# Zero fills of a results' array, two per iteration of the first attention and each behind that iteration's reciprocal

## The chip, the cores and the metric

The kernel runs on one core of a Trainium2 chip. The time is the device time of one execution in microseconds (us), and the median of several executions is compared. Before the change it is 1532.57 us, the median of three runs (1531.0 to 1534.91).

The engines go by short names. PE is the matrix engine TensorE, and PEld its weight loads. DVE is VectorE, ACT is ScalarE, POOL is GpSimd. SP is the engine that issues the plain DMA transfers here, and SPq is its queue of instructions. Each engine carries out its own instructions in order; engines wait for each other through semaphores.

## The reference, cut to what matters

The model has two layers, each an attention over another sequence and then a mixture of 8 experts in which every token goes to its two best ones. The batch has 64 entries of 128 tokens with 128 features.

```python
x = x + L0_xattn(layernorm(x), fside, memory_k=ctx, memory_v=ctx)   # 16 heads of 8, keys: 128 + 120
x = x + L0_ffn(layernorm(x))          # router, top 2 of 8 experts, silu(a) * g @ w2
x = x + L1_xattn(layernorm(x), ctx, ctx)                            # 16 heads of 8, keys: 120
x = x + L1_ffn(layernorm(x))          # router, top 2 of 8 experts, gelu
...
# the first mixture of experts
for e in range(E):
    he = silu(a) * g @ w2[e].T
    out = out + where(expert_ids == e, he, 0)
combined = (out * scores).reshape(N, TOP_K, h).sum(axis=1)
```

Everything is computed in 32-bit floats.

## The kernel before, in words

**Stages.** The profile's first 640 us are the first attention. Then come some 350 us in which the first mixture of experts is worked off in 71 tiles of 256 rows (NTL is 71), and then the second attention, with the second mixture of experts woven in.

**The first attention.** One iteration `it` handles one batch entry at each of several stages: maxima of the scores for entry `it` (L394 on PE, L414 on DVE), the scores again and their exponentials for entry `it - 2` (L430 on PE, L438 on ACT), the values for entry `it - 3` (L475), and the division and output projection for entries `it - 3` to `it - 5`. Near the end of an iteration `out2` (L487) turns the values of one entry round on PE (L491), takes the reciprocals of the sums on DVE (L495) and multiplies (L497). So there is one such reciprocal in each iteration from `it = 3` on. In each iteration PE does all the L394 and L430 products before the turn at L491.

**Groups and loads.** Four entries make a group `g`. The key tiles `K2` exist twice, for even and odd groups. The context half of the keys of group `g` is written there by two loads at L261 of 240 KB each, in the program at iteration `4(g-1) + 2`. It overwrites what group `g - 2` used, and group `g - 2` is last read by the L394 and L430 products of iteration `4(g-1) + 1`. It is first read by L394 in iteration `4g`. The context half of the values follows at L266 (960 KB), and the next source of keys and values, `kvT`, at L256 (256 KB).

**The results' array.** `ys` lies in the chip's main memory and takes the results of the 71 expert tiles (L1135), which are later gathered by row (L1157, L1360). Before that, each of its 71 pieces of 256 rows is filled with zeros from the tile `zero` by a DMA of 128 KB (L1278). `Aside0.end`, called last in every iteration, writes two such fills into the program from `it = 4` to `it = 39`.

**The order of work.** PE, ACT, DVE and POOL work in the order in which the program was written. In the first attention's first 62 iterations this isn't so for SP:

```python
with tc.manual_schedule(engines=ORDERED):    # L1328; ORDERED: PE, ACT, DVE, POOL
    for _ in range(B - 2):
        next(steps)
```

There the framework's planner sets SP's order before the kernel runs. It goes by when, on its own estimate of times, the things that a transfer waits for are done. On the chip SP then keeps to that order: a transfer that waits holds all later ones. In the last iterations (L1331) SP's order too is as written. The framework finds most waits from the tiles that an instruction reads and writes. The tile `zero` is set once at the start, and `ys` isn't read or written by anything before the fills, so that the fills before the change wait for nothing in the attention.

Of the kernel before, what the change touches and what calls it, by code (L numbers as in the profile page):

```python
# [23 lines left out]
HD = 8  # L24
# [20 lines left out]
def transformer_kernel(ctx, tc, a, out):  # L45
    nc = tc.nc
# [185 lines left out]
    def attention(layer, w, norm, first, aside):  # L232
# [5 lines left out]
        with ExitStack() as es:  # L238
# [37 lines left out]
            def mtile():  # L276
                return banks.tile([128, 512], F32, name="bank", tag="bank")
# [209 lines left out]
            def out2(b):  # L487
                ov = ots.pop(b)
                pt = mtile()
                for v in range(NV):  # L490
                    nc.tensor.transpose(pt[:, v * 128 : (v + 1) * 128], ov[:, v * S : (v + 1) * S], ident)  # L491
                pt = pt[:, : NV * 128].rearrange("q (h w) -> q h w", w=16)
                rs = stat.tile([S, H], F32, name="rs", tag="rs")
                aside.probe = rs[0:1, 0:1]
                nc.vector.reciprocal(rs, pt[:, :, HD])  # L495
                o = rows.tile([S, H, HD], F32, name="o", tag="o")
                nc.vector.tensor_tensor(  # L497
                    o, pt[:, :, 0:HD], rs.unsqueeze(2).to_broadcast([S, H, HD]), ALU.mult
                )
                pts[b] = o  # L500
# [52 lines left out]
            for it in range(B + 5):  # L553
# [21 lines left out]
                if first:  # L575
# [13 lines left out]
                    rounds(2, 3)  # L589
                    on(4, out3)  # L590
                    on(3, out2)
                    prep(it, 1)
                    aside.end(it, work, mtile)
                else:
# [5 lines left out]
                    prep(it, 0)  # L600
                    on(4, out3)
                    on(3, out2)
                    on(5, out4)
                    aside.call(it, mtile)
# [20 lines left out]
    class Router:  # L625
# [22 lines left out]
        def rest(self, mtile):  # L648
            self.mtile = mtile
            self.t = 1 << 20  # L650
            while min(self.due) < 1 << 30:
                self.call(None, mtile)
# [52 lines left out]
        def best(self, lg, n, l):  # L705
# [26 lines left out]
            nc.vector.tensor_scalar(cap, one1, -BIG, BIG / 2.0, ALU.mult, ALU.add)  # L732
            rest = tl("rest", n)
            nc.vector.tensor_tensor(rest, lg, cap, ALU.min)
            nc.vector.tensor_reduce(m2, rest, AX.X, ALU.max)
            yield 0
            one2 = first_at(rest, m2, "one2")
            yield 0
            e2 = tl("e2", n, 1)
# [503 lines left out]
    class Aside0(Ahead):  # L1243
# [29 lines left out]
        def end(self, it, work, mtile):  # L1273

            for t in range(2 * (it - GB), 2 * (it - GB) + 2):

                if 0 <= t < NTL:
                    nc.sync.dma_start(  # L1278
                        ys[t * TT : (t + 1) * TT].rearrange("(h p) d -> p h d", p=S), zero[:, :, :D]
                    )  # L1280
            if it == B - 2:
                self.tiles = tile_stage(work, mtile)
            if it >= B - 2:
                next(self.tiles)

        def rest(self, mtile):
            for _ in self.tiles:
                pass


    wr0 = const.tile([D, 3 * E], F32, name="c_wqkvT", tag="c_wqkvT")
# [270 lines left out]
```

## Time and profile before

| What | us |
|---|---|
| median of three runs | 1532.57 |
| the profiled execution's own time | 1582.29 |
| its span, first to last instruction | 1580.5 |
| PE busy | 1442.8 (91% of the span) |
| DVE busy | 1106.3 (70%) |
| ACT busy | 849.7 (54%) |
| POOL busy | 641.3 (41%) |

The profiled execution is 3.2% longer than the median of the unprofiled runs. Times of rows are counted from the span's start. A row names the line, the engine, the operation, the tile that it writes and those that it reads. For a DMA issued by SP the row gives the time that SP spent on issuing it; the transfer itself runs on afterwards. A wait is put down to the work whose end came last. The granted clock of PE (PEclk) is a share of full speed.

### The profile page before, as it was taken

What the parts mean: (1) busy time and instruction counts of PE and PEld (TensorE: products, weight loads), DVE (VectorE), ACT (ScalarE), POOL (GpSimd) and SP (SyncE); (2) the same over time, 40 slices, a digit from 0 to 9 for tenths busy, and PEclk for the clock granted to TensorE, in tenths of its full rate; (3) what the DMA queues carried; (4) which work ended last, traced back from release to release, by engine and by line L of the source; (5) the groups of instructions that cost most, each with busy time, mean ns of one, the idle gap of its engine ahead of it and who ended that gap; (6) DMA issues with size and microseconds to landing.
All of it is one profiled execution on the core that took longest, in us unless ns stands there. A gap on an engine that the chain in (4) does not pass through costs nothing.

```text
span 1580.5 us, 41996 instructions
## 1 busy us (share of the span) xinstructions
PE 1442.8 (91%) x16620; PEld 1118.6 (71%) x16620; DVE 1106.3 (70%) x3024; ACT 849.7 (54%) x1740; POOL 641.3 (41%) x1195
## 2 busy tenths in 40 slices
PE   7969999999999999787999999888989898988987
PEld 5757777777777677676888888566666676666765
DVE  6757888888888988354654444688776777777763
ACT  4646666666666666442333333566656565655653
POOL 4122345646465534464001122376555555444210
PEclk9989999999999999899999999899999999999999
DMA  7851222222222221365776676111000111100000
GB/s 192 222 138 46 55 61 68 67 61 64 57 64 58 56 70 37 93 187 173 213 201 189 194 202 180 46 35 30 28 28 28 37 31 31 31 28 15 15 8 28
DMA packets 143719, 133.03 MB, mean 84 GB/s; under 512 B 48546, under 2 KB 126114, under 8 KB 141602
## 3 DMA queue, kind: packets, MB, share of 16 engines
q1 hardware_dynamic: 135330, 113.02, 25.9%
q0 software_dynamic: 8192, 17.32, 3.5%
q8 instruction: 132, 2.16, 0.6%
q14 instruction: 65, 0.53, 0.1%
HBM read 97.32 MB, written 32.97 MB: 82 GB/s over the span
## 4 chain that ended last, share of the span: by engine, by line
PE 66%; DVE 15%; DMA 6%; SPq 5%; issue 3%; ACT 3%; POOL 3%; another core or an unknown queue 0%; POOLq 0%; ACTq 0%; DVEq 0%
PE bank L430 10%; PE bank L475 9%; PE bank L1115 8%; PE bank L394 8%; PE bank L1420 4%; PE bank L1441 4%; DVE nm L414 3%; PE bank L1128 3%; DMA q<-xs 3%; SPq L1278 2%; PE bank L407 2%; PE bank L292 2%; DVE q L462 2%; PE bank L511 2%; PE bank L681 2%
## 5 line engine op out<-in xcount | busy, mean ns | idle before, releaser
L414 DVE TENSOR_REDUCE nm<-bank 128x2 f32<-128x496 f32 (+1 forms) x768 | 465.4, 662 | 100.6 <-PE bank L430 68.6
L438 ACT ACTIVATE p<-bank 120x512 f32<-120x512 f32 (+1 forms) x768 | 403.5, 603 | 154.9 <-PE bank L430 138.5
L430 PE MATMUL bank<-q,k 32*120 32x256 f32 (+1 forms) x3072 | 444.5, 401 | 14.8 <-DVE nm L414 5.0
L430 PEld LDWEIGHTS bank<-q,k 32*120 32x120 f32 (+1 forms) x3072 | 298.3, 182 | 61.9 <-DVE nm L414 16.6
L394 PE MATMUL bank<-k,q 32*128 32x248 f32 x2048 | 294.3, 403 | 12.5 <-DMA k<-in_ctx_k 11.8
L394 PEld LDWEIGHTS bank<-k,q 32*128 32x128 f32 x2048 | 203.1, 190 | 59.7 <-issue 23.0
L475 PE MATMUL bank<-p,v 128*32 128x128 f32 (+1 forms) x4096 | 179.6, 279 | 1.8 <-DVE h L1435 0.6
L1120 DVE TENSOR_TENSOR p<-p,bank 128x256 f32<-128x256 f32 x213 | 87.9, 420 | 125.4 <-ACT p L1119 112.6
L407 PE MATMUL bank<-k,qf 32*128 32x480 f32 x512 | 150.8, 604 | 1.3 <-ACT qf L295 0.8
L807 POOL DMA_INDIRECT xs<-xn,at x128 | 129.2, 1009 | 28.6 <-issue 25.0
L1119 ACT ACTIVATE p<-bank 128x256 f32<-128x256 f32 x213 | 80.9, 384 | 100.9 <-PE bank L1115 91.9
L484 ACT COPY ov<-bank 128x256 f32<-128x256 f32 x128 | 48.0, 375 | 157.5 <-PE bank L475 146.0
L475 PEld LDWEIGHTS bank<-p,v 128*32 128x32 f32 (+1 forms) x4096 | 111.2, 110 | 26.1 <-issue 13.2
L1115 PE MATMUL bank<-q 128*128 128x256 f32 x516 | 122.3, 388 | 4.6 <-ACT q L1106 4.6
L1360 POOL DMA_INDIRECT yb<-ys,back x112 | 108.7, 970 | 27.7 <-issue 19.3
L462 DVE SCALAR_TENSOR_TENSOR q<-bank,c_smask,q 128x256 f32<-128x256 f32 x256 | 111.1, 475 | 10.3 <-PE bank L459 9.6
L167 POOL TENSOR_SCALAR xn<-x,mv,rstd 128x128 f32<-128x128 f32 x252 | 110.6, 452 | 7.3 <-issue 1.3
L1115 PEld LDWEIGHTS bank<-q 128*128 128x128 f32 x516 | 97.4, 196 | 17.3 <-ACT q L1106 5.0
L155 POOL TENSOR_SCALAR rstd<-mv 128x4 f32<-128x4 f32 x32 | 6.4, 199 | 246.7 <-DVE mv L113 150.0
L475 PE MATMUL bank<-p,vc 120*32 120x128 f32 x2048 | 104.2, 272 | 0.6 <-issue 0.5
L1157 POOL DMA_INDIRECT kvT<-ys,back x16 | 15.4, 962 | 197.5 <-DMA vc<-xs 118.1
L301 ACT ACTIVATE q<-bank,c_a_bq,c_hmask 128x512 f32<-128x512 f32 x124 | 90.1, 788 | 9.8 <-PE bank L292 9.8
(224 smaller groups left out, 2477.6 us busy)
## 6 DMA issues: line engine op xcount, KB each, us to landing
q<-in_w SPq DMA_DIRECT2D x43, 576.0 KB
vc<-in_w SPq DMA_DIRECT2D x28, 576.0 KB
vc<-in_ctx_v SPq DMA_DIRECT2D x16, 960.0 KB
ys<-zero SPq DMA_DIRECT2D x71, 128.0 KB
k<-in_ctx_k SPq DMA_DIRECT2D x32, 240.0 KB
q<-xs SPq DMA_DIRECT2D x43, 128.0 KB
ys<-q SPq DMA_DIRECT2D x43, 128.0 KB
x<-in_x SPq DMA_DIRECT2D x16, 256.0 KB
```

The source lines that it names most:

```text
L167: nc.gpsimd.tensor_scalar(xn[:, j, :D], xg[g][:, j, :], self.mv[:, b, 0:1], self.rstd[:, b : b + 1], ALU.add, ALU.mult,)
L301: nc.scalar.activation(q4s[g][:, :, s, :], pq.rearrange("p (b q) -> p b q", b=GB), AF.Identity, bias=w["bq"][:, s : s + 1], scale=hmask[:, ...
L394: nc.tensor.matmul(pa[:, u, :], lhsT=q4s[g][r, j, s, :], rhs=k2[g % 2][r, s // 2, j, :], start=True, stop=True,)
L407: lambda: nc.tensor.matmul(pa, lhsT=qfs[g][r, j, :], rhs=k4s[g][r, :, j, :], start=True, stop=True),
L414: nc.vector.tensor_reduce(nm[b % 2].rearrange("q i (a s) -> q a i s", s=16)[:, 2 * ra + v : 2 * ra + v + len(slots) // 2, :, 0], pa.rearra ...
L430: nc.tensor.matmul(pb[:n, v * 256 : (v + 1) * 256], lhsT=k2[g % 2][r, v, j, k0 : k0 + n], rhs=q4s[g][r, j, 2 * v : 2 * v + 2, :].rearrange ...
L438: nc.scalar.activation(ps_[b][:n, c, ra, :], pb[:n], AF.Exp, scale=SCALE)
L462: nc.vector.scalar_tensor_tensor(q, pm, smask[:, v : v + 1], q, ALU.mult, ALU.add)
L475: nc.tensor.matmul(pav[32 * ra : 32 * ra + 32, v * S : (v + 1) * S], lhsT=vs[g % 2][c][:, j, 4 * v + ra, i, :], rhs=p[:n, c, ra, (2 * v + ...
L807: s = nc.gpsimd.indirect_dma_start(xs, bass.IndirectOffsetOnAxis(at[:, j, k : k + 1], 0), xn, None)
L1115: nc.tensor.matmul(ph[:, u, :], lhsT=w[:, c, u * 128 : (u + 1) * 128], rhs=xT, start=True, stop=True)
L1360: nc.gpsimd.indirect_dma_start(y[:, k, b % 2, :], None, ys, bass.IndirectOffsetOnAxis(back[:, b, k : k + 1], 0),)
```

## The change

The reciprocal of `out2` is remembered in `aside.pace`. Each fill of `ys` is given a dependency on the reciprocal remembered last, which is that of its own iteration, since `out2` comes before `end` in an iteration. The fills, their number, their sizes and their place in the program stay as they are. The dependency is of the kind that puts a real wait into the program.

```diff
@@ out2 @@
                 aside.probe = rs[0:1, 0:1]
-                nc.vector.reciprocal(rs, pt[:, :, HD])
+                aside.pace = nc.vector.reciprocal(rs, pt[:, :, HD])
@@ Aside0.end @@
                 if 0 <= t < NTL:
-                    nc.sync.dma_start(
+                    z = nc.sync.dma_start(
                         ys[t * TT : (t + 1) * TT].rearrange("(h p) d -> p h d", p=S), zero[:, :, :D]
                     )
+
+                    tc.add_manual_dep(z.ins, self.pace.ins.name, AFTER, reason="spread")
@@ after the class @@
+    AFTER = mybir.DependencyInfo(mybir.DependencyClass.Sync, mybir.DependencyReason.DATA)
```

## The prediction

> **What bounds the kernel now.** I read the stretches first, to see which engine fills the first attention and where it doesn't. Columns: busy us of each engine (instructions), granted clock, DMA share, GB/s.
>
> ```profile
> 40.00:84.00 44.00, 42.08 (x651) 31.25 (x642) 30.94 (x68) 28.51 (x58) 5.46 (x14) 0.96 0.80 218
> 84.00:96.00 12.00, 0.36 (x4) 0.39 (x8) 0.70 (x3) 0.58 (x2) 0.00 (x0) 0.68 0.84 234
> 96.00:110.00 14.00, 13.69 (x177) 10.19 (x173) 9.55 (x20) 9.51 (x18) 4.18 (x13) 0.91 0.35 85
> 110.00:400.00 290.00, 285.24 (x4409) 216.96 (x4410) 242.10 (x596) 184.76 (x374) 136.54 (x309) 1.00 0.23 59
> ```
>
> PE is busy for 98% of 110 to 400 us, so PE bounds the attention. But from 84 to 96 us PE, DVE and ACT all stand still while the DMA engines move 234 GB/s. The waits up to 110 us say for what (total us, times, longest us):
>
> ```profile
> PE bank L394 <- DMA k<-in_ctx_k: 11.8, 1, 11.8
> ```
>
> One wait, for the context keys of the third group (g = 2, first used in iteration 8). PE's timeline gives its place, and shows the matmuls slow behind it (0.75 us here, 0.47 us for the first ones at 80.69 us):
>
> ```profile
> 83.23 0.63 PE L176 MATMUL bank<-ident,xn 128*128 128x128 f32 x4
> 95.64 0.75 PE L394 MATMUL bank<-k,q 32*128 32x248 f32 x1 [11.78 <-DMA k<-in_ctx_k]
> ```
>
> SP's timeline says why the keys were late (start, us of issuing, count):
>
> ```profile
> 39.71 0.37 SPq L256 DMA_DIRECT2D kvT<-in_fsideT  x1
> 40.31 11.81 SPq L1278 DMA_DIRECT2D ys<-zero  x8
> 52.24 0.39 SPq L256 DMA_DIRECT2D kvT<-in_fsideT  x1
> 52.67 39.79 SPq L1278 DMA_DIRECT2D ys<-zero  x63
> 92.56 1.04 SPq L261 DMA_DIRECT2D k<-in_ctx_k  x2
> ...
> 114.63 0.92 SPq L261 DMA_DIRECT2D k<-in_ctx_k  x2
> ```
>
> All 71 zero fills, which nothing holds, stand in one block in front of the keys' load. SP needs 39.79 us to issue the last 63 (0.63 us each), and PE runs dry before SP is through. Last, what the gap costs in full, by the reciprocals on DVE, one per iteration (here those of iterations 7, 8, 9, 10, 11, 12):
>
> ```profile
> 84.16 0.25 DVE L495 RECIPROCAL rs<-bank 128x16 f32<-128x16 f32 x1
> 106.39 0.25 DVE L495 RECIPROCAL rs<-bank 128x16 f32<-128x16 f32 x1
> 116.40 0.24 DVE L495 RECIPROCAL rs<-bank 128x16 f32<-128x16 f32 x1
> 125.24 0.24 DVE L495 RECIPROCAL rs<-bank 128x16 f32<-128x16 f32 x1
> 133.94 0.24 DVE L495 RECIPROCAL rs<-bank 128x16 f32<-128x16 f32 x1
> 143.35 0.25 DVE L495 RECIPROCAL rs<-bank 128x16 f32<-128x16 f32 x1
> ```
>
> Iteration 8, which opens a group, takes 106.39 - 84.16 = 22.23 us; iteration 12, which opens the next and waits for no load, takes 143.35 - 133.94 = 9.41 us. The gap costs **22.23 - 9.41 = 12.82 us**: 11.78 us of waiting and 1.04 us of something else.
>
> **What the 1.04 us is.** The granted clock of 84 to 96 us is 0.68 and of the next 14 us 0.91: PE comes out of the gap at half speed. The Trainium skill (TensorE: Matmul & The Clock Gate, Part 1) says that an idle window of about 3.4 us halves the clock and that about 3.4 us of sustained work restore it; 3.4 us at half speed would lose 1.7 us. That is an estimate from the page; the sum would be 11.78 + 1.7 = 13.5 us by it and 12.8 us by the reciprocals. I take the measured 12.8, which already holds what the engines catch up after a stop.
>
> **The change part by part.** *The block of fills dissolves.* Each fill now waits for its iteration's reciprocal. The keys of g = 2 are free to be overwritten once iteration 5's last L394 and L430 products are done, which on PE stand before the turn that feeds that iteration's reciprocal (66.61 us). For g = 3 the same order shows in the rows: load at 114.63, reciprocal of iteration 9 at 116.40, 1.77 us later. So the load of g = 2 can go at about 66.61 - 1.8 = 64.8 us. It took 2.94 us from first issue to landing in the chain of waits (amid the fills), so it lands near 68 us; PE wants it at 83.86 us. Cover: 16 us. The wait goes, and with it the low clock: **-12.8 us**. What is late next at that place? DVE's and ACT's last rows before the gap end at 84.7 and 84.6 us, under a microsecond after PE's, and iteration 12 has the same neighbours and takes 9.41 us with them; so nothing takes the gap's place, and the 9.41 already contains that lag.
>
> *Issuing the fills, two by two.* 71 issues at the median 0.50 us (fastest 0.36) are some 36 us of SP, spread over 36 iterations (reciprocals at 58.04 to about 399 us): 1 us in each 9.4. In this stretch SP issues four loads per group of 38 us, under 2 us, and stands idle otherwise. Cost 0. Without that cover each pair would cost 1 us, 36 us in all.
>
> *The transfers.* A fill moves 131 KB; at the 218 GB/s of 40 to 84 us that is 0.6 us, 1.2 us per pair, 28 GB/s over an iteration, beside 59 GB/s at a DMA share of 0.23. A load that meets a pair lands 1.2 us later, against 16 us of cover: 0. POOL's scatters (L807, from 226.5 us) share the DMA engines but not SP's queue; nothing waits for them in their rows: 0.
>
> *DVE.* The reciprocal itself is unchanged. Signalling it to SP costs between nothing (its end is already counted for POOL, which waits for the same result at L806) and one extra semaphore event of 21 ns, as ten of these reciprocals carry already: 36 x 0.021 = 0.8 us at most. DVE isn't the bound; I take 0.
>
> *The first real write of `ys`* (L1135) comes at 660.68 us, some 260 us after the last fill: 0.
>
> Sum in the profiled execution: 1580.5 - 12.8 = **1567.7 us of span**, 1569.5 of own time. The attention behind the gap is a chain bound by PE with loads that follow PE's progress, and the expert tiles follow the attention; nothing later waits for a fixed time, so the gain arrives at the end. Later stages drop to half clock now and then; their shift against these windows may give or take about 3 us (my allowance: two windows of 3.4 us at half speed).
>
> **From the profile to the runs.** The median is 0.9686 of the profiled time. If everything shrinks alike, the gain is 12.4 us. The gap is a race between SP and PE, and the profile may slow the two differently, so I bound it. If only PE is quicker unprofiled, it wants the keys at 83.86 x 0.9686 = 81.2 us and they land at 95.5: a gap of 14.3 us, gain 15.3 with the clock. If only SP is quicker, by 63 x 0.08 us (0.55 us between two fills down to the 0.47 us seen between other issues) and by the four longer pauses in the block (4 x 1.3 us), the keys land near 85.3 us: a gap of 1.5 us, gain 1.5. Between such ends I stay near the row: 12 us, so **1520.5 us**.
>
> **The rivals.**
>
> *Smaller gap unprofiled (0.15).* As just bounded, half-way to the lower end: gain 2 to 8 us, 1524 to 1531. For it: the block's pace is partly that of issuing, which a profile could stretch. Against it: the DMA engines show 0.80 busy at 218 GB/s, so transport isn't far behind as a limit.
>
> *Nothing gained (0.06).* Another wait stands where this one stood, or the fills still come bunched: within 1528 to 1537. Against it: DVE and ACT end within a microsecond of PE, and iterations 9 to 12 show no PE wait.
>
> *Slower (0.10): a fill at the head of SP's queue holds the keys.* The Trainium skill (DMA: Bandwidth & Descriptors, Anatomy of one DMA) says that DMA engines don't wait on semaphores: the wait happens on the issuing sequencer. This speaks against the change, and the trace agrees: SP waited 26.7 us at a stretch for PE with L261 and issued nothing meanwhile. If the planner puts the keys of group g behind the fills of iteration 4g - 1, they go only after its reciprocal: for g = 2 that is 84.16 + 0.25, two issues of 0.5, 2.94 to land: 88.3 us against 83.86, a gap of 4.5 us, plus about 1 us of low clock, at nine group openings (it = 8 to 40): 9 x 5.5 = 50, less 12.8: +37 us, 1569. It decides from 12.8 / 9 = 1.4 us lost per opening. One iteration earlier, behind the fills of 4g - 2 (75.46 + 4.2 = 79.7 us), the keys are still in time. Against it: to stand that far back the planner would have to believe a reciprocal of iteration 4g - 1 done before products that PE does two iterations earlier, which the written order of PE excludes unless SP is backed up in its reckoning. The placing of the 63 fills before the keys is, though, a sign that its reckoning isn't the chip's.
>
> **How the numbers follow.** Full gain 0.69 (own range 1515.5 to 1525), smaller gap 0.15, nothing 0.06, slower 0.10. A measurement of this kernel tells 0.3%, 4.6 us, from no change. The full gain and two thirds of the smaller-gap case lie beyond it: faster 0.79; the rest of that case and "nothing": same 0.11; slower 0.10. The range 1515 to 1530 takes the full case nearly whole and most of the smaller-gap case, and leaves about 2 in 10 out.
>
> **What would show it.** Right: in the profile after, no wait of L394 for `k`; reciprocals 7 to 8 about 9.4 us apart; granted clock 1.0 from 52 to 640 us; fills in pairs from about 58 to 386 us, each just behind a reciprocal; keys of g = 2 issued near 65 us; span near 1568. Wrong: SP rows of L261 that follow a fill instead of PE's products, repeated PE waits for `k`, `vc` or `kvT` at group openings; or no gap, but a median that moved less than the span, which would be the profile's own doing.

## The result

The kernel after takes **1517.32 us** (median of four runs, 1514.49 to 1520.04) against 1532.88 us before (four runs, 1531.0 to 1534.91): a ratio of 0.9898 with a 95% interval of 0.9875 to 0.9922, so 15.6 us less (12 to 19 by the interval). The prediction said 1520.5 us, range 1515 to 1530.

The first four experiments below ran on one chip and the last four on another, where every kernel, the kernel before included, took some 50 us longer, as did the execution profiled ahead of the prediction (span 1580.5 us); so each kernel is compared with the kernel before of its own set, and the times expected for the last four are to be read as differences from it.

The stretches of the kernel after, with the same borders as before the change (columns as there: busy us of PE, PEld, DVE, ACT and POOL, granted clock, DMA share, GB/s):

```profile
40.00:84.00 44.00, 42.21 (x652) 31.25 (x640) 31.02 (x68) 28.81 (x57) 5.44 (x14) 0.96 0.44 105
84.00:96.00 12.00, 11.69 (x168) 8.33 (x166) 8.98 (x20) 9.01 (x18) 4.16 (x13) 1.00 0.15 45
96.00:110.00 14.00, 14.00 (x250) 11.83 (x253) 10.14 (x26) 6.56 (x15) 5.43 (x14) 1.00 0.30 77
110.00:400.00 290.00, 286.37 (x4422) 217.04 (x4418) 246.16 (x609) 188.53 (x382) 140.07 (x322) 1.00 0.32 84
```

From 84 to 96 us PE was busy for 0.36 us before and is busy for 11.69 us now, at full clock. The bytes that left 40 to 84 us (218 to 105 GB/s) and 84 to 96 us (234 to 45 GB/s) turn up after 110 us (59 to 84 GB/s), where PE is as busy as it was. SP's timeline of the kernel after (start, us of issuing, count):

```profile
57.95 0.89 SPq L1278 DMA_DIRECT2D ys<-zero  x2
64.48 0.93 SPq L261 DMA_DIRECT2D k<-in_ctx_k  x2
66.53 0.88 SPq L1278 DMA_DIRECT2D ys<-zero  x2
70.66 0.36 SPq L266 DMA_DIRECT2D vc<-in_ctx_v  x1
75.37 0.88 SPq L1278 DMA_DIRECT2D ys<-zero  x2
76.34 0.46 SPq L256 DMA_DIRECT2D kvT<-in_fsideT  x1
```

The keys of the third group go at 64.48 us instead of 92.56 us, two microseconds ahead of the fills of iteration 5. The reciprocals of iterations 7, 8, 11 and 12 on DVE:

```profile
83.80 0.25 DVE L495 RECIPROCAL rs<-bank 128x16 f32<-128x16 f32 x1
93.20 0.25 DVE L495 RECIPROCAL rs<-bank 128x16 f32<-128x16 f32 x1
...
120.77 0.25 DVE L495 RECIPROCAL rs<-bank 128x16 f32<-128x16 f32 x1
130.17 0.25 DVE L495 RECIPROCAL rs<-bank 128x16 f32<-128x16 f32 x1
```

Iteration 8 now takes 9.40 us, like iteration 12 (9.40 us); it took 22.23 us. Of PE's waits up to 110 us for a transfer only the one at the very start is left, which both kernels have:

```profile
PE bank L202 <- DMA kvT<-in_fsideT: 5.8, 1, 5.8
```

### The profile page after: what moved, and what is told of

Same layout as the page of the kernel before. It is cut to its first block, busy times and chain, and to the rows that moved or that the text cites. A ratio compares the mean times of both kernels' runs of the same rounds, so it can differ in the third digit from the quotient of the medians.

```text
span 1514.3 us, 42033 instructions
## 1 busy us (share of the span) xinstructions
PE 1421.0 (94%) x16620; PEld 1107.5 (73%) x16620; DVE 1102.4 (73%) x3024; ACT 847.6 (56%) x1740; POOL 640.4 (42%) x1195
## 4 chain that ended last, share of the span: by engine, by line
PE 69%; DVE 15%; DMA 4%; POOL 4%; ACT 4%; issue 2%; SPq 1%; POOLq 0%; DVEq 0%; ACTq 0%
PE bank L430 11%; PE bank L394 10%; PE bank L475 9%; PE bank L1115 9%; PE bank L1424 4%; PE bank L1445 4%; DVE nm L414 4%; PE bank L1128 3%; DMA q<-xs 2%; PE bank L407 2%; PE bank L214 2%; DVE q L462 2%; PE bank L511 2%; PE bank L681 2%; PE bank L202 2%
## 5 line engine op out<-in xcount | busy, mean ns | idle before, releaser
L430 PE MATMUL bank<-q,k 32*120 32x256 f32 (+1 forms) x3072 | 438.1, 399 | 11.4 <-DVE nm L414 5.2
L430 PEld LDWEIGHTS bank<-q,k 32*120 32x120 f32 (+1 forms) x3072 | 293.5, 181 | 56.8 <-DVE nm L414 17.3
L394 PE MATMUL bank<-k,q 32*128 32x248 f32 x2048 | 291.0, 399 | 0.7 <-ACT q L334 0.5
L394 PEld LDWEIGHTS bank<-k,q 32*128 32x128 f32 x2048 | 202.2, 189 | 47.9 <-issue 11.0
L475 PE MATMUL bank<-p,v 128*32 128x128 f32 (+1 forms) x4096 | 175.6, 275 | 0.2
L1115 PE MATMUL bank<-q 128*128 128x256 f32 x516 | 118.6, 379 | 1.6 <-ACT q L1106 1.6
```

The lines of the kernel that those rows point to most:

```text
L394: nc.tensor.matmul(pa[:, u, :], lhsT=q4s[g][r, j, s, :], rhs=k2[g % 2][r, s // 2, j, :], start=True, stop=True,)
L430: nc.tensor.matmul(pb[:n, v * 256 : (v + 1) * 256], lhsT=k2[g % 2][r, v, j, k0 : k0 + n], rhs=q4s[g][r, j, 2 * v : 2 * v + 2, :].rearrange ...
L475: nc.tensor.matmul(pav[32 * ra : 32 * ra + 32, v * S : (v + 1) * S], lhsT=vs[g % 2][c][:, j, 4 * v + ra, i, :], rhs=p[:n, c, ra, (2 * v + ...
L1115: nc.tensor.matmul(ph[:, u, :], lhsT=w[:, c, u * 128 : (u + 1) * 128], rhs=xT, start=True, stop=True)
```

## The experiments

**The kernel before once more**, unchanged, for a second profile.

> The kernel before, unchanged, for a second profile. Its first profile had a span of 1580.5 us against a median of 1532.9 us, while the profile of the kernel after has 1514.3 us against 1517.3. Theory A (profiling costs next to nothing, and the first profile fell on an unusually slow execution): a span within 1528 to 1540 us, with the one PE wait for the context keys of the third group still in it, 11 to 14 us long. Theory B (profiling slows this kernel by 3%): a span near 1580 us again.

Measured: 1537.3 us, span 1535.5 us, in a set where the kernel before has a median of 1535.99 us. So profiling costs next to nothing here, and the 3.2% between the first profile and the first median had another origin (the last section says what is known of it). Here PE's timeline and DVE's reciprocals of iterations 7 and 8 show:

```profile
96.90 0.75 PE L394 MATMUL bank<-k,q 32*128 32x248 f32 x1 [12.83 <-DMA k<-in_ctx_k]
```

```profile
84.38 0.25 DVE L495 RECIPROCAL rs<-bank 128x16 f32<-128x16 f32 x1
108.74 0.25 DVE L495 RECIPROCAL rs<-bank 128x16 f32<-128x16 f32 x1
```

Iteration 8 takes 24.36 us, which is 14.95 us over the 9.41 us of iteration 12: 12.83 us of waiting and 2.12 us behind it. The stretches of this run show PE's clock behind the wait:

```profile
84.00:88.90 4.90, 0.08 (x1) 0.00 (x0) 0.92 (x3) 0.80 (x3) 0.00 (x0) 0.98 0.75 216
88.90:102.60 13.70, 5.70 (x59) 4.66 (x63) 3.19 (x6) 2.17 (x4) 0.00 (x0) 0.51 0.87 218
102.60:110.00 7.40, 7.09 (x110) 4.88 (x99) 4.13 (x11) 5.18 (x10) 4.16 (x13) 1.00 0.03 10
```

The granted clock of 88.9 to 102.6 us is 0.51. By the clock records it is one half from 88.70 to 102.35 us, so PE's first 5.45 us after the wait (96.90 to 102.35 us) run at half speed. In the profile ahead of the prediction this lasted only from 95.64 to 98.66 us, 3.0 us, and 1.04 us were lost. The two go together in all the traces kept here: in the fourteen gaps at a group opening (nine of them in one experiment below) PE works 2.87 to 6.19 us at half clock, and the time lost behind the wait grows with it throughout, from 0.96 to 2.49 us.

**The whole block behind one reciprocal.** All 71 fills stay together, but behind iteration 5.

```diff
-            for t in range(2 * (it - GB), 2 * (it - GB) + 2):
+            for t in range(NTL) if it == GB + 1 else ():
```

> All 71 fills in one block as before, but the whole block behind the reciprocal of iteration 5, thus just behind the keys of the third group in SP's queue. Theory A (what cost the time was the block's place in SP's queue, ahead of the keys): no PE wait for those keys, time as the kernel after, 1514 to 1521 us; the block runs from about 66 to 109 us and the loads behind it (context values of group 2, keys of group 3) are issued near 110 us, just in time for iterations 11 and 12, so at most 2 us are lost there. Theory B (what cost the time was the bunching, the load on the DMA engines): 1526 to 1534 us, with waits at other places.

Measured: 1526.69 us against 1535.99 us for the kernel before in the same set, a ratio of 0.9933 (0.9916 to 0.995). The wait for keys is gone, as theory A had it, but the loss elsewhere isn't within 2 us. The time, and a wait at another place, are what theory B had. SP's timeline, and PE's:

```profile
64.39 0.93 SPq L261 DMA_DIRECT2D k<-in_ctx_k  x2
66.44 46.89 SPq L1278 DMA_DIRECT2D ys<-zero  x71
113.42 0.46 SPq L266 DMA_DIRECT2D vc<-in_ctx_v  x1
```

```profile
120.86 0.66 PE L475 MATMUL bank<-p,vc 120*32 120x128 f32 x8 [5.13 <-DMA vc<-in_ctx_v]
```

The block took 46.89 us instead of the 43 that I had reckoned with, the context values behind it (960 KB) went at 113.42 us, PE could use them 7.4 us later, and iteration 11 waits 5.13 us for them. It takes 16.10 us instead of 8.71: 7.4 us lost, about half of the gain. Theory B's numbers came true, but its reason (the load on the DMA engines) isn't needed for them: the values took about their usual time once issued (median 7.3 us, see the next experiment), against 42.8 us that they were issued later than in the kernel after (70.66 us). It is SP's queue that holds the load; in both of its places a block of this length stood ahead of a load, and moving it only chose which.

**A shorter block.** Only pieces 60 to 70 are held.

```diff
-                    tc.add_manual_dep(z.ins, self.pace.ins.name, AFTER, reason="spread")
+                    if t >= 60:
+                        tc.add_manual_dep(z.ins, self.pace.ins.name, AFTER, reason="spread")
```

> Only the fills of pieces 60 to 70 are held behind their reciprocals; the other 60 stay in a block before the keys. Theory A (a race between SP's block and PE): the block is shorter by 11 x 0.63 = 6.9 us, the wait for the keys falls from 11.8 to about 4.9 us, some low clock remains; time 1523 to 1527 us. Theory B (any block before the keys costs the same, for instance through the clock): 1530 to 1535 us.

Measured: 1528.22 us, a ratio of 0.994 (0.9922 to 0.9958) to before, 7.8 us less; that is 1.2 us above theory A's range and below theory B's. PE's waits:

```profile
PE bank L394 <- DMA k<-in_ctx_k: 5.9, 1, 5.9
```

Against the second profile of the kernel before, in the same set, the wait is 12.8 - 5.9 = 6.9 us shorter for 11 fills fewer, as reckoned; the 5.9 us that are left are 1.0 us more than expected, because the reckoning started from the 11.8 us of the first profile, and the kernel before is itself 3.1 us longer in this set than beside the result (1535.99 against 1532.88 us). It is a race, and each fill in the block costs its own length once the race is lost.

The same trace settles whether the fills, besides holding the keys back, also slow their transfer. The chain of waits gives the keys' time from issue to landing right behind the block (85.51 us), and the profile's page the medians of all such loads whose landing it shows (last column, us):

```profile
85.51 3.01 DMA k<-in_ctx_k
```

```profile
vc<-in_ctx_v SPq DMA_DIRECT2D x16, 960.0 KB, 7.3
k<-in_ctx_k SPq DMA_DIRECT2D x32, 240.0 KB, 3.3
```

Behind 60 fills the keys took 3.01 us, against a median of 3.3 us. What the block costs is the time until the load is issued, not a slower transfer.

**The slower rival: keys behind the fills of iteration 4g - 1.** The kernel after, with the keys of groups 2 to 10 written later and held by that iteration's reciprocal.

```diff
             def context_k(g):
                 for v in range(NV):
-                    nc.sync.dma_start(
+                    k = nc.sync.dma_start(
...
+                    if 2 <= g <= 10:
+                        tc.add_manual_dep(k.ins, aside.pace.ins.name, AFTER, reason="late")
...
                 if first:
-                    context_k(g)
+                    if not 2 <= g <= 10:
+                        context_k(g)
                     context_v(g)
...
                     aside.end(it, work, mtile)
+                    if it % GB == 3 and 2 <= it // GB + 1 <= 10:
+                        context_k(it // GB + 1)
```

> The kernel after, but the context keys of groups 2 to 10 are written into the program at the end of iteration 4g - 1 and wait for its reciprocal: the rival of the prediction, made on purpose. Theory A (the rival's price as worked out: 4.5 us of PE wait and about 1 us of low clock at each of nine group openings): 50 us above the kernel after, 1560 to 1575 us, with nine PE waits for keys. Theory B (a key load lands faster than the 2.94 us seen amid the fills, or PE has other work to do): 2 us or less per opening, 1525 to 1535 us.

Measured: 1581.78 us against 1535.99 us before, a ratio of 1.03 (1.028 to 1.032). PE's waits (the line is L394 of the other kernels):

```profile
PE bank L397 <- DMA k<-in_ctx_k: 43.3, 9, 5.3
```

The time is 6.8 us above the range expected. There are nine waits of 4.8 us on average, where 4.5 was reckoned. The iterations that open a group take 15.23 to 16.50 us instead of 9.41, 60.1 us more in all. So each opening costs 6.7 us: 4.8 of waiting and (60.1 - 43.3) / 9 = 1.9 us behind it, where 1 was reckoned; the trace's clock records show the half clock at each of the nine. The mechanism of the rival is real and dear. It didn't come about, because the planner put each load ahead of the fills of its own iteration.

**Written later, without a wait.** The kernel before, its fills in iterations 24 to 59 of the program.

```diff
-            for t in range(2 * (it - GB), 2 * (it - GB) + 2):
+            for t in range(2 * (it - 24), 2 * (it - 24) + 2):
```

> The kernel before, its fills still waiting for nothing, but written into the program 20 iterations later (iterations 24 to 59). Theory A (only a real wait moves the fills; the planner sends what has nothing to wait for as soon as it reaches it, wherever it is written): the block still stands ahead of the keys of the third group, a PE wait of 12 to 13 us, time 1530 to 1538 us. Theory B (the later place alone spreads them): 1514 to 1521 us.

Measured: 1584.75 us against 1583.0 us before in this set, a ratio of 1.0 (0.9981 to 1.0018), theory A. SP's timeline and PE's wait:

```profile
40.87 52.62 SPq L1278 DMA_DIRECT2D ys<-zero  x71
93.59 1.04 SPq L261 DMA_DIRECT2D k<-in_ctx_k  x2
```

```profile
PE bank L394 <- DMA k<-in_ctx_k: 14.0, 1, 14.0
```

The place in the program is worth nothing: fills with nothing to wait for are sent from 40.87 us on when they are written in iterations 24 to 59, as from 40.31 us on when they were written in iterations 4 to 39.

**Eight per iteration.**

```diff
-            for t in range(2 * (it - GB), 2 * (it - GB) + 2):
+            for t in range(8 * (it - GB), 8 * (it - GB) + 8):
```

> The kernel after, with eight fills per iteration instead of two (iterations 4 to 12), each eight behind their iteration's reciprocal. Theory A (what counts is that no load is passed by more fills than its slack has room for): eight issues take about 4 to 5 us of SP, a load behind them still lands an iteration early, time as the kernel after, 1514 to 1521 us, no PE wait for keys or values. Theory B (the number two matters, through the load on the DMA engines): waits for k or vc at iterations 8 to 13 and 1522 to 1530 us.

Measured: 1567.46 us against 1583.0 us before in this set, a ratio of 0.9892 (0.9865 to 0.9918), the same gain as with two. SP's timeline:

```profile
64.57 1.25 SPq L261 DMA_DIRECT2D k<-in_ctx_k  x2
66.61 5.66 SPq L1278 DMA_DIRECT2D ys<-zero  x8
72.37 0.46 SPq L266 DMA_DIRECT2D vc<-in_ctx_v  x1
```

A load is held up by 5.66 us at most, and PE waits for no key and no value. The difference to before is the one expected.

**The fills from ACT**, two per iteration in ACT's written order, no wait added.

```diff
-                    nc.sync.dma_start(
+                    nc.scalar.dma_start(
```

> The fills issued by ACT instead of SP, two per iteration in ACT's written order, with no wait added. Theory A (SP's queue is what was blocked): the keys are issued near 65 us, no PE wait for them, 1514 to 1522 us; ACT pays about 1 us per iteration for issuing, which it has, being busy 6 of 9.4 us. Theory B (ACT's issuing delays the exponentials that PE waits for): iterations 4 to 39 grow by up to 1 us each, up to 1550 us.

Measured: 1567.73 us against 1583.0 us, a ratio of 0.9888 (0.9858 to 0.9917): the same gain without any wait, theory A, since the fills now stand in the queue of an engine that works in program order. The keys go at 64.94 us, and iterations 4 to 12 take to 0.02 us what they take in the kernel after (iteration 8: 9.41 us), so ACT's two issues of some 0.4 us disturb nothing there.

**The fills in halves**, 142 of 64 KB, none held.

```diff
-                    nc.sync.dma_start(
-                        ys[t * TT : (t + 1) * TT].rearrange("(h p) d -> p h d", p=S), zero[:, :, :D]
-                    )
+                    for h in range(2):
+                        r = t * TT + h * S
+                        nc.sync.dma_start(ys[r : r + S], zero[:, h, :D])
```

> The kernel before, each fill split into two of 64 KB, none held: the same bytes in 142 issues. The planner puts 99 of them ahead of the keys' first load. Theory A (the block's pace is set by issuing, about 0.55 us each): the 83 halves behind the kvT load take 46 us, the keys are issued near 98 us instead of 93, PE waits about 17 us, time 1535 to 1543 us. Theory B (the pace is set by bytes, some 0.63 us per 128 KB): the 83 halves take 26 us, the keys are issued near 79 us and PE waits 2 us at most: 1517 to 1523 us.

Measured: 1590.74 us against 1583.0 us, a ratio of 1.0036 (1.0019 to 1.0053). SP's timeline and PE's wait:

```profile
55.67 43.78 SPq L1280 DMA_DIRECT2D ys<-zero  x83
99.54 0.38 SPq L261 DMA_DIRECT2D k<-in_ctx_k  x1
```

```profile
PE bank L394 <- DMA k<-in_ctx_k: 18.9, 1, 18.9
```

The 83 halves take 43.78 us where theory A had 46 and theory B 26, and the wait is 18.9 us where theory A had 17. A fill of half the bytes costs 43.78 / 83 = 0.53 us in the block, a whole one 0.63 to 0.65 us in a block of 63 (39.79 / 63 and, in the second profile, 41.21 / 63) and up to 0.74 us in one of 71 (52.62 / 71). So the block's length goes mostly by the number of issues, theory A; but not by it alone, since two fills of the kernel after, with no other fills around them, take 0.88 us, 0.44 each. What adds the rest was not separated.

## Why the prediction was right

*The cause.* The block of fills ahead of the keys in SP's queue: shown, by the shorter block (6.9 us of wait for 11 fills), by the fills on ACT (gain without any wait) and by the place in the program that changed nothing. Traffic on the DMA engines is not needed to explain it: behind 60 fills the keys landed in 3.01 us, no later after their issue than usual.

*The keys' new time and its cover.* Reckoned to go at 64.8 us, they go at 64.48 us. That nothing is late next at this place was right: iteration 8 takes 9.40 us.

*Two fills per iteration cost nothing.* Right. With two, with eight, or on another engine, the gain is the same within its interval, and iterations 9 to 12, which in the kernel before had no fills beside them, take in the kernel after the same times to 0.01 us (10.02, 8.84, 8.71 and 9.40 us against 10.01, 8.84, 8.70 and 9.41).

*The low clock: mis-sized.* I took the measured 1.04 us of one gap over the 1.7 us that I had estimated from the Trainium skill (TensorE: Matmul & The Clock Gate, Part 1). The second profile has 2.12 us and the nine forced waits 1.9 us each; by these the estimate was nearer. But its ground, some 3.4 us of work that restore the clock, isn't what the gaps show: PE worked between 2.87 and 6.19 us at half speed. One occurrence was too little to size this term (the last section has what the clock records show).

*From the profile to the runs: this step was wrong.* I supposed that profiling makes the execution 3.2% longer, scaled the 12.8 us down by it and took 12. The second profile lasts as long as an ordinary run. Read from that one, the sum would have been 12.83 + 2.12 = 14.95 us, and the 15.6 us measured agree with it. The predicted 12 us lie just at the end of the measured interval (12 to 19 us). They were short by the mis-sized clock (1.1 us), by a wait that was 1.0 us longer in the second profile than in the first, and by the scaling (0.8 us). The span of 1568 us foretold for the profile after is 1514.3 us for the same reason: the first profile was of a longer execution. Against the second profile (1535.5 us) that span is 21.2 us shorter; 15.5 us of this are there by the end of the first attention, the rest arises in the later stages and was not traced.

*The rivals.* The slower one was priced at 37 us over before and takes 45.8; its waiting was right (4.8 us for 4.5), its clock term too small again. The planner put each load ahead of its iteration's fills, as argued. The smaller gap outside the profile didn't occur.

## What to carry to other kernels

Work that waits for nothing isn't free when it shares an in-order queue with loads that do wait: a planner that sends by readiness sends all of it at once, ahead of the next load, and writing it later in the program doesn't help. Tie it to the progress of the compute, or put it on a queue that already works in program order; the exact number per step (two or eight here) doesn't matter while a load's slack exceeds what may go ahead of it. Before scaling a profile to the runs, look whether the profiled execution itself is ordinary: a second profile would have given the whole gain here.

## What was not expected of the hardware

The same kernel before took about 1535 us on the chip of the first experiments and 1583 us on that of the later ones, and the profile ahead of the prediction, whose chip is not known, looks like the latter. Its trace spreads the difference over the whole kernel (iterations of 9.9 us where the second profile has 8.8, again and again from 275 us on, then more in the later stages), with the same instructions at nearly the same durations. Whether the chip itself or something else made the difference was not tried, and its cause stays open. The gain is 15 to 16 us at both levels (0.9898 for the kernel after at one, 0.9892 and 0.9888 for its two relatives at the other).

By the clock records, the half clock comes in periods that are whole multiples of 3.41 us (3.4 to 20.5 us long, apart from a last one that ends with the record), and within each trace all changes of the clock lie whole multiples of 3.41 us apart. So how long PE stays slow after a wait depends on where between two such times it restarts: in the second profile of the kernel before it restarted at 96.90 us and the half clock ended at 102.35 us, in the first at 95.64 and 98.66 us.
